# Router logits of the last three tiles as matmuls, and a new order of work between attention and experts

## The chip, the core and the metric

The kernel runs on one core of a Trainium2 chip. A core has five engines, each with its own instruction stream: TensorE (PE, matmuls and transposes, results into PSUM), VectorE (DVE), ScalarE (ACT), GpSimd (POOL) and SyncE (SP, which here only issues transfers). They run in order and meet only through semaphores; transfers issued by SP, ACT or POOL run on 16 shared DMA engines. The metric is device time in microseconds (us), lower is better, and each kernel is run several times.

## What is computed

A gated cross-attention block followed by a mixture of experts: 4 x 2048 tokens of width 512, 16 heads over a context of 77 rows, then for each token the two best of ten experts (eight true ones and two that give nothing).

```python
x = x + tanh(g_xattn) * xattn(layernorm(x), ctx)        # softmax(q k^T) v, w_out, times tanh(gate)
h = layernorm(x)
logits = h @ gate_w.T + gate_b                          # [tokens, 10]
weights, selected = top_k(softmax(logits), 2)
norm_w = weights * (selected < 8), divided by their sum
out = sum over the chosen experts e of norm_w * (h @ expert_w[e] + expert_b[e])
x = x + tanh(g_ffn) * out
```

## The kernel before

Tokens are cut into 64 tiles of 128 (`NT`), 16 tiles to a batch. After a setup the work has two phases, and the order of instructions on every engine is the order in which the Python code emits them (`manual_schedule`).

**Phase 1, attention.** `step(i)` is run for i from -4 to 62 and holds pieces of several tiles: `scores` of tile i+1 (PE), `softmax_exp` and `softmax_div` of it, the transposition of its attention weights by 32 x 32 squares on DVE (`attn_squares`) and by 16 transfers on SP (`attn_move`, line 353), `attend` of tile i-1 (PE, line 360: ten matmuls of 128 x 512 into `po`), its residual x1 (`residual`, written out by SP at line 374), the second layer norm (`norm_stats`, `norm_root`, `norm_shift`, `norm_apply`, which leaves h in a row buffer `rows[i % 9]`), and the router of tile i-2: `gate_logits` makes ten logits by ten DVE instructions at line 382, each a product of h with one broadcast row of `gwb` and a sum; `choose` finds the two best (lines 410 to 423), `ratio` gets their weight (an Exp on ACT, line 430), and on every second tile `weigh`, `place` and `dispatch` count places by two small matmuls (line 453) and scatter the finished rows (512 values of h, two weights, the token number) into two DRAM buffers `hb`, sorted by expert, with four indirect transfers on POOL (line 475).

**Phase 2, experts.** The rows are read back in 118 slots (`M`): 51 blocks and 8 partial sets in pass 0 (first choices), the same number in pass 1 (second choices). `order[n]` holds (pass, table, index); a table of None is a partial set of one expert, gathered by POOL (line 881). A slot goes through

- `slot_load`: read the row block into one of 11 ring buffers, as five transfers on SP, or on SP and ACT from slot 9 on (lines 902 and 905); the address comes from a table in SBUF, `starts`;
- `slot_acc`: gather the present outputs of the slot's tokens (POOL, line 925);
- `slot_tr`: transpose the rows, for a block by one DVE instruction (line 943) into one of six buffers `hTs`, for a partial set by an ACT copy, four PE transposes and another ACT copy (lines 952 to 958), which take two of the same six buffers;
- `slot_pe`: four f32 products with the expert's weights (line 981; the expert's number is read from the table `which`), 8 records in the trace;
- `slot_out`: add the bias, multiply by the weight, add to the gathered output (DVE, lines 989 and 990);
- `slot_put`: scatter the result to the output (POOL, line 997).

Products go to PSUM tiles from two pools of three buffers: even slots to `px`, odd ones to `pe` (pool `mm`, which `po`, the count matmuls `pp` and `pc` also use).

Three tables (`early_table`, `first_table`, `second_table`) say where the blocks of the first 16 slots, of the rest of pass 0 and of pass 1 begin, and `part_table` gives the partial sets.

**The passage** stands at the end of the code. When tile 63's scores are through, PE still has `attend(62)` and `attend(63)`, and the router has tiles 61, 62 and 63 to do. The code emits products 0 and 1, then for each of the two last tiles: gate logits of the tile before on DVE, `attend`, `choose`, residual, norm; then the loop over q = 1..118, which puts out slot q-1, loads slot q+5, transposes slot q+2, and does product and output of slot q. `tail(q)`, at the end of each turn, spreads tile 63's ten gate logits over turns 0 to 4, its `choose` at 5, its dispatch and the first table at 8, the second table at 12, the partial table at 14.

## Time and profile before

| | us |
|---|---|
| median of 8 runs | 1697.81 |
| lowest, highest | 1696.51, 1700.73 |
| the profiled execution, as timed | 1700.13 |
| its span from first to last instruction | 1698.4 |
| PE busy in it | 1645.3 (97%) |
| DVE busy | 1292.6 (76%) |
| ACT busy | 884.2 (52%) |
| POOL busy | 465.6 (27%) |
| PE on the chain that ended last | 85% |

The profile is one execution as the hardware profiler took it. A busy share is the part of the span in which an engine had an instruction running. The chain of waits is followed back from the last instruction: at each step to what released it, or to the instruction before it on its engine. In a timeline, a line gives start, length, engine, source line, operation, the tile that is written and those that are read, how many instructions of one kind were merged, and in brackets the idle time before it with what seems to have ended it. The granted clock is the share of full speed that TensorE's throttle let through. Attention lasts until about 1223 us of the span; the expert products run from there to 1688 us, and the last scatter ends the span.

### The profile page before, as it was taken

What the parts mean: (1) busy time and instruction counts of PE and PEld (TensorE: products, weight loads), DVE (VectorE), ACT (ScalarE), POOL (GpSimd) and SP (SyncE); (2) the same over time, 40 slices, a digit from 0 to 9 for tenths busy, and PEclk for the clock granted to TensorE, in tenths of its full rate; (3) what the DMA queues carried; (4) which work ended last, traced back from release to release, by engine and by line L of the source; (5) the groups of instructions that cost most, each with busy time, mean ns of one, the idle gap of its engine ahead of it and who ended that gap; (6) DMA issues with size and microseconds to landing.
All of it is one profiled execution on the core that took longest, in us unless ns stands there. A gap on an engine that the chain in (4) does not pass through costs nothing.

```text
span 1698.4 us, 23173 instructions
## 1 busy us (share of the span) xinstructions
PE 1645.3 (97%) x4530; PEld 812.8 (48%) x4530; DVE 1292.6 (76%) x3324; ACT 884.2 (52%) x3188; POOL 465.6 (27%) x617
## 2 busy tenths in 40 slices
PE   8898999999999999999999999999978999999996
PEld 6544455454545455454545455454433444444443
DVE  1553899898998989898998989899987564466553
ACT  2564777777776777777776777777510000100001
POOL 4031111121111111121111211121146556465563
PEclk9999999999999999999999999999989999999998
DMA  7477443346533435543333666665467885578751
GB/s 241 169 203 206 113 97 88 87 108 152 152 88 92 106 93 144 149 107 90 93 87 93 166 158 157 154 167 134 95 168 214 248 234 179 154 231 250 232 182 55
DMA packets 484934, 252.07 MB, mean 148 GB/s; under 512 B 369509, under 2 KB 425829, under 8 KB 484529
## 3 DMA queue, kind: packets, MB, share of 16 engines
q1 hardware_dynamic: 423473, 134.77, 33.9%
q0 software_dynamic: 34528, 103.55, 18.6%
q10 hardware_dynamic: 26784, 12.20, 2.9%
q14 instruction: 109, 0.89, 0.2%
q8 instruction: 40, 0.66, 0.2%
HBM read 119.41 MB, written 100.52 MB: 129 GB/s over the span
## 4 chain that ended last, share of the span: by engine, by line
PE 85%; DVE 5%; issue 3%; DMA 2%; SPq 2%; ACT 1%; another core or an unknown queue 1%; DVEq 0%; POOL 0%; POOLq 0%; ACTq 0%
PE po L360 29%; PE sc L281 29%; PE pe L981 11%; PE px L981 10%; PE pkv L519 2%; DVE prod L382 2%; PE xtr L261 2%; PE pv L622 2%; DMA vw_all<-row 1%; SPq L353 1%; DMA gwb<-in_L_ffn_gate_w_dram 1%; PE pm L597 0%; DVE acc L990 0%; PE str L957 0%
## 5 line engine op out<-in xcount | busy, mean ns | idle before, releaser
L360 PE MATMUL po<-vw,aT 128*128 128x512 f32 (+1 forms) x1280 | 562.9, 595 | 5.7 <-DVE attn L327 5.4
L281 PE MATMUL sc<-m_sb,xnT 128*128 128x385 f32 (+1 forms) x1536 | 552.9, 510 | 0.0
L382 DVE CUSTOM_DVE_ANT_0 prod<-row,gwb,gbias 128x512 f32<-128x512 f32 x640 | 477.9, 747 | 24.0 <-DMA gwb<-in_L_ffn_gate_w_dram 6.2
L360 PEld LDWEIGHTS po<-vw,aT 128*128 128x128 f32 (+1 forms) x1280 | 244.3, 191 | 309.0 <-issue 301.7
L281 PEld LDWEIGHTS sc<-m_sb,xnT 128*128 128x128 f32 x1536 | 283.9, 190 | 212.5 <-issue 86.1
L475 POOL DMA_INDIRECT hb<-row,dst x128 | 128.8, 1006 | 752.6 <-DVE nbh_h L250 673.7
L314 ACT ACTIVATE attn<-sc,nmx 128x77 f32<-128x77 f32 x1024 | 316.0, 347 | 33.3 <-DVE nmx L309 27.7
L314 ACT ACTIVATION_READ_ACCUMULATOR attn<-sc,nmx 128x1 f32 x1024 | 233.2, 228 | 0.0
L981 PE MATMUL px<-big,m_sb 128*128 (+1 forms) x472 | 215.8, 600 | 11.7 <-issue 10.3
L981 PE MATMUL pe<-big,m_sb 128*128 (+1 forms) x472 | 217.8, 605 | 5.2 <-DVE m_sb L943 4.2
L981 PEld LDWEIGHTS px<-big,m_sb 128*128 128x128 f32 x472 | 90.1, 193 | 123.3 <-issue 120.4
L981 PEld LDWEIGHTS pe<-big,m_sb 128*128 128x128 f32 x472 | 90.9, 195 | 117.6 <-issue 112.1
L303 DVE TENSOR_REDUCE mx<-sc 128x5 f32<-128x385 f32 (+1 forms) x192 | 106.2, 580 | 19.2 <-PE sc L281 17.1
L233 ACT ACTIVATE sdh_h<-mvh_h,eps_t 128x1 f32<-128x1 f32 x64 | 18.9, 295 | 191.9 <-DVE rsa_a L245 182.6
L989 DVE TENSOR_TENSOR yb<-px,blks 128x512 f32<-128x512 f32 x59 | 40.4, 686 | 92.3 <-issue 45.8
L989 DVE TENSOR_TENSOR yb<-pe,blks 128x512 f32<-128x512 f32 x59 | 40.5, 686 | 79.7 <-issue 37.6
L952 ACT COPY m_sb<-row 128x512 f32<-128x512 f32 x11 | 6.8, 620 | 177.4 <-DVE acc L990 174.3
L997 POOL DMA_INDIRECT out_dram<-acc,row x75 | 76.3, 1018 | 79.2 <-DVE acc L990 54.4
L264 ACT ACTIVATE xnT<-xtr,bet,gam 128x128 f32<-128x128 f32 x256 | 95.4, 452 | 4.5 <-PE xtr L261 4.5
L327 DVE TENSOR_TENSOR attn<-attn,ri 128x1232 f32<-128x1232 f32 x64 | 92.3, 1442 | 5.1 <-DMA aT<-attn 0.8
L373 DVE SCALAR_TENSOR_TENSOR x<-po,gx,x 128x512 f32<-128x512 f32 x64 | 48.0, 750 | 62.7 <-PE pp L453 36.0
L336 DVE STREAM_TRANSPOSE attn<-attn 128x1248 f32<-128x1248 f32 x64 | 94.1, 1471 | 0.0
(163 smaller groups left out, 1539.4 us busy)
## 6 DMA issues: line engine op xcount, KB each, us to landing
aT<-attn SPq DMA_DIRECT2D x768, 40.0 KB
x<-in_x_dram SPq DMA_DIRECT2D x64, 256.0 KB
out_dram<-x SPq DMA_DIRECT2D x64, 256.0 KB
aT<-attn SPq DMA_DIRECT2D x256, 36.0 KB
row<-hb SPq DMA_DIRECT2D x138, 64.0 KB
big<-in_L_ffn_expert_w_dram SPq DMA_DIRECT2D x32, 256.0 KB
row<-hb ACTq DMA_DIRECT2D x118, 64.0 KB
vw<-vw_all SPq DMA_DIRECT2D x9, 768.0 KB
```

The lines of the kernel that those rows point to most:

```text
L264: nc.scalar.activation(xnT[:, c, :], ptr[:, c, :], AF.Identity, bias=bet[:, c : c + 1], scale=gam[:, c : c + 1],)
L281: nc.tensor.matmul(t[:, : n1 - n0], xnTs[i][:, c, :], m_sb[:, c, n0:n1], start=(c == 0), stop=(c == NC - 1),)
L303: nc.vector.tensor_reduce(mx[:, g0:g1], scs[i, g][:, : (g1 - g0) * SK].rearrange("p (h k) -> p h k", k=SK), AX.X, ALU.max,)
L314: nc.scalar.activation(a[:, h * SK : (h + 1) * SK], t[:, k : k + SK], AF.Exp, bias=nm[:, h : h + 1], scale=SCALE, accum_out=sm[:, h : h + 1],)
L327: nc.vector.tensor_tensor(a, a, ri.unsqueeze(2).to_broadcast([P, H, SK]), ALU.mult)
L336: nc.vector.transpose(a[:, :n], a[:, :n])
L360: nc.tensor.matmul(po, aT[:m, k, :], vw[:m, k, :], start=(k == 0), stop=(k == NKC - 1),)
L382: nc.vector.tensor_tensor_reduce(prod, hrs[i][:, :D], gwb[:, e, :], 1.0, gbias[:, e : e + 1], ALU.mult, ALU.add, pgs[i][:, e : e + 1],)
L475: ins = nc.gpsimd.indirect_dma_start(out=hb[k], out_offset=bass.IndirectOffsetOnAxis(ap=dst[:, i % 2, k : k + 1], axis=0), in_=hr[:, :].bi ...
L981: nc.tensor.matmul(pe, hsT[:, c, :], w[:, c, :], start=(c == 0), stop=(c == NC - 1))
L989: nc.vector.tensor_tensor(tt, pe, b, ALU.add)
L997: ins = nc.gpsimd.indirect_dma_start(out=of, out_offset=bass.IndirectOffsetOnAxis(ap=tok, axis=0), in_=acc, in_offset=None, bounds_check=T ...
```

## The change

Six things are changed; phase 1 up to step 61 stays as it was but for one small load and four transposes.

1. `setup_gate` (at step 4): the gate weights, loaded once more as ten rows by SP, are transposed by four small PE transposes and copied to `gwT`. The logits of tiles 61, 62 and 63 are made by `gate_transpose` (four PE transposes of h, one ACT copy to `hgT`) and `gate_product` (four PE products of 10 columns, one DVE instruction that adds the bias) in place of ten DVE instructions for each.
2. The 16 transfers of tile 63's attention weights go alternately to SP and ACT.
3. Row blocks are loaded 8 slots ahead in the loop in place of 5, blocks are transposed 5 slots ahead in place of 2; partial sets still 2 ahead, but into six buffers of their own, `hPs`, in the space of `gwb`.
4. Products 0 to 2 go to `px`, 3 to 5 to `pe`, and so on in threes; the counts `pp` and `pc` of the passage use the transposes' PSUM tiles.
5. In the passage products 1 to 5 stand between the gate steps; all routing of tile 63 is emitted before the output of slot 0, its four scatters one behind each of the outputs 1 to 4 in the program (`later`).
6. The tables are made at turns 3, 6 and 9 in place of 8, 12 and 14.

```diff
-    def attn_move(i, n0=0, n1=16):
-        for dst, src in moves[i][n0:n1]:
-            nc.sync.dma_start(dst, src)
+    def attn_move(i, n0=0, n1=16, queues=(nc.sync,)):
+        for n, (dst, src) in enumerate(moves[i][n0:n1]):
+            queues[n % len(queues)].dma_start(dst, src)
...
+    def setup_gate():
+        rows10 = rows[NRB - 1][:, :D]
+        ptr = tr_tile("gwtr")
+        for c in range(NC):
+            nc.tensor.transpose(ptr[:, c, :NG], rows10[:NG, c * P : (c + 1) * P], ident[:NG, :NG])
+        nc.vector.tensor_copy(gwT, ptr[:, :, :NG])
+
+    def gate_transpose(i):
+        ptr = tr_tile(f"gtr{i}")
+        for c in range(NC):
+            nc.tensor.transpose(ptr[:, c, :], hrs[i][:, c * P : (c + 1) * P], ident)
+        nc.scalar.copy(hgT, ptr)
+
+    def gate_product(i):
+        pl = tr_tile(f"gl{i}")[:, 0, :NG]
+        for c in range(NC):
+            nc.tensor.matmul(pl, hgT[:, c, :], gwT[:, c, :], start=(c == 0), stop=(c == NC - 1))
+        pgs[i] = stile("pg", i, NG)
+        nc.vector.tensor_tensor(pgs[i], pl, gbias, ALU.add)
...
-            attn_move(i + 1)
+            attn_move(i + 1, queues=(nc.sync, nc.scalar) if i + 1 == NT - 1 else (nc.sync,))
...
-        hp, hsT = (hTs[(turn[1] + k) % len(hTs)] for k in range(2))
-        turn[1] += 2
+        hp, hsT = (hPs[(turn[2] + k) % len(hPs)] for k in range(2))
+        turn[2] += 2
...
-        if n % 2:
+        if n // 3 % 2:
             pe = mm_tile(f"pe{n}")
...
     def tail(q):
-        i = NT - 1
-        if q < 5:
-            gate_logits(i, 2 * q, 2 * q + 2)
-        elif q == 5:
-            choose(i)
-            ratio(i)
-        elif q == 8:
-            weigh(i // 2)
-            place(i // 2)
-            pc = count_rows(csum[0][:, 0])
-            dispatch(i // 2)
-            first_table(pc)
-        elif q == 12:
+        if 0 < q <= len(later):
+            put_rows(*later[q - 1])
+        if q == 3:
+            first_table(count_rows(csum[0][:, 0], flat_tr("pclast")))
+        elif q == 6:
             second_table()
-        elif q == 14:
+        elif q == 9:
             part_table()
...
+        nc.sync.dma_start(rows[NRB - 1][:NG, :D], gate_w)
         for i in range(1, NT - 1):
...
-            if i == NT - 2:
-                slot_load(3)
-                slot_load(4)
+            if i == 4:
+                setup_gate()
             step(i)
...
-        slot_load(5)
+        for n in range(3, 6):
+            slot_load(n)
         slot_pe(0)
-        slot_pe(1)
-        slot_tr(2)
-        slot_tr(3)
+        for n in range(1, 3):
+            slot_tr(n)
         for i in (NT - 2, NT - 1):
-            gate_logits(i - 1, 0, NG)
             attend(i)
-            choose(i - 1)
-            ratio(i - 1)
+            gate_transpose(i - 1)
             residual(i)
             norm_stats(f"h{i}", x1s[i])
             norm_root(f"h{i}")
-            if i == NT - 2:
-                weigh(i // 2 - 1)
-                place(i // 2 - 1)
-                dispatch(i // 2 - 1)
+            slot_pe(i - NT + 3)
+            gate_product(i - 1)
             norm_shift(f"h{i}")
             hrs[i] = rows[i % NRB]
             norm_apply(f"h{i}", hrs[i][:, :D], x1s.pop(i))
+            choose(i - 1)
+            ratio(i - 1)
             if i == NT - 2:
-                slot_pe(2)
-                slot_load(6)
+                weigh(i // 2 - 1)
+                place(i // 2 - 1, flat_tr("pp"))
+                dispatch(i // 2 - 1)
+                slot_tr(3)
+                for n in range(6, 9):
+                    slot_load(n)
         for n in range(4):
             slot_acc(n)
-        tail(0)
+        i = NT - 1
+        slot_pe(3)
+        gate_transpose(i)
+        slot_tr(4)
+        slot_pe(4)
+        gate_product(i)
+        choose(i)
+        ratio(i)
+        slot_tr(5)
+        slot_pe(5)
+        weigh(i // 2)
+        place(i // 2, flat_tr("pplast"))
+        dispatch(i // 2, later)
         slot_out(0)
         for q in range(1, M + 1):
-            if 1 < q < M - 5:
-                slot_load(q + 5)
+            if q < M - 8:
+                slot_load(q + 8)
             slot_put(q - 1)
...
-            if 1 < q < M - 2:
-                slot_tr(q + 2)
-            if 2 < q < M:
+            for n, whole_tile in ((q + 5, True), (q + 2, False)):
+                if n < M and whole_tile == (order[n][1] is not None):
+                    slot_tr(n)
+            if 5 < q < M:
                 slot_pe(q)
             if q < M:
                 slot_out(q)
             tail(q)
```

More of the change, by code (lines that the diff above doesn't have):

```diff
@@ L459, in place, with dispatch @@
             )
-    def dispatch(m):
+    def dispatch(m, later=None):
         pos, pp = poss.pop(m), pps.pop(m)
@@ L773, with count_rows @@
     ]
[L774 to L778 removed]
+    hPs = [gwb[:, n, :].rearrange("p (c k) -> p c k", k=P) for n in range(6)]
+    hgT = m_flat[:, 6 * D : 7 * D].rearrange("p (c k) -> p c k", k=P)
+    scr = m_flat[:, 7 * D :]
+    assert NT * (2 * NE + 1) <= NC * COLS - 7 * D
+    def count_rows(cs, pc=None):
+        pc = mm_tile("pc") if pc is None else pc
         nc.tensor.matmul(
```

46 lines of the change are left out of this document (25 added, 21 removed).

## The prediction

> **What bounds the kernel now.** First I read busy time by stretch: start and end in us, length, busy us of TensorE (PE), its weight loads, VectorE (DVE), ScalarE (ACT), GpSimd (POOL), granted clock, DMA share, GB/s.
>
> ```profile
> 1240.00:1260.00 20.00, 15.54 (x36) 6.37 (x34) 14.64 (x47) 5.23 (x8) 8.38 (x8) 0.97 0.53 147
> 1260.00:1280.00 20.00, 14.25 (x30) 6.29 (x31) 18.21 (x39) 1.58 (x2) 14.50 (x14) 0.77 0.76 226
> 1280.00:1300.00 20.00, 19.04 (x48) 8.32 (x47) 16.09 (x39) 0.00 (x0) 13.55 (x14) 1.00 0.79 233
> 1300.00:1350.00 50.00, 45.75 (x100) 19.82 (x99) 31.06 (x57) 0.00 (x0) 27.94 (x28) 0.93 0.83 236
> 1350.00:1500.00 150.00, 145.21 (x358) 65.11 (x357) 76.62 (x113) 9.23 (x16) 88.97 (x87) 0.99 0.66 193
> 1500.00:1650.00 150.00, 150.00 (x357) 66.78 (x356) 90.58 (x132) 1.72 (x3) 95.48 (x92) 1.00 0.78 228
> 1650.00:1698.00 48.00, 35.11 (x93) 16.28 (x91) 12.99 (x18) 7.21 (x13) 21.21 (x21) 0.87 0.23 70
> ```
>
> PE is full from 200 to 1220 us and from 1500 to 1650. So only PE's own work, its idle time and its slow clock set the end. Idle time sits in the passage (1238 to 1311), around 1440 and 1484, and near the end. The PE timeline (start, length, instructions, idle time before) names the places:
>
> ```profile
> 1214.20 8.75 PE L360 MATMUL po<-vw,aT 128*128 128x512 f32 x20
> 1222.79 3.60 PE L981 MATMUL px<-big,m_sb 128*128 x8
> 1252.15 3.60 PE L981 MATMUL pe<-big,m_sb 128*128 x8
> 1265.75 4.51 PE L981 MATMUL px<-big,m_sb 128*128 x6 [10.00 <-issue]
> 1311.06 6.60 PE L981 MATMUL pe<-big,m_sb 128*128 x8 [4.25 <-DVE m_sb L943]
> 1446.21 0.75 PE L957 MATMUL str<-ident,m_sb 128*128 128x128 f32 x4 [2.42 <-ACT m_sb L952]
> 1446.75 5.25 PE L981 MATMUL px<-big,m_sb 128*128 128x512 f32 x8
> 1486.04 3.70 PE L981 MATMUL px<-big,m_sb 128*128 x8 [1.38 <-DVE acc L990]
> 1659.38 1.11 PE L957 MATMUL str<-ident,m_sb 128*128 128x128 f32 x4 [3.52 <-ACT m_sb L952]
> ```
>
> A po, the output of one attention tile, takes 8.59 us from start to start; a slot's product (8 matmuls) 3.43. Wait A is 10.0 us before product 4, wait C 4.25 before product 15, D 2.42 (with 0.99 at 1439.69) and F 3.52 before transposes of partial slots, E 1.38 before product 62. After A, C, D and F the clock is low: product 15 takes 6.44 us start to start. What A and C wait for stands in DVE's timeline:
>
> ```profile
> 1257.12 0.69 DVE L989 TENSOR_TENSOR yb<-px,blks 128x512 f32<-128x512 f32 x1
> 1260.41 0.75 DVE L990 SCALAR_TENSOR_TENSOR acc<-yb,row,acc 128x512 f32<-128x512 f32 x1 [2.60 <-DMA acc<-out_dram,row]
> 1262.80 0.81 DVE L990 SCALAR_TENSOR_TENSOR acc<-yb,row,acc 128x512 f32<-128x512 f32 x1 [0.91 <-DMA acc<-out_dram,row]
> 1264.99 0.71 DVE L943 STREAM_TRANSPOSE m_sb<-row 128x512 f32<-128x512 f32 x1
> ...
> 1305.10 0.75 DVE L990 SCALAR_TENSOR_TENSOR acc<-yb,row,acc 128x512 f32<-128x512 f32 x1
> 1310.12 0.20 DVE L816 TENSOR_SCALAR which<-m_sb 128x64 int32<-128x64 f32 x1
> 1310.29 0.71 DVE L943 STREAM_TRANSPOSE m_sb<-row 128x512 f32<-128x512 f32 x1
> ```
>
> Slot 4's transpose (1264.99) stands behind the outputs of slots 0 and 1, which wait for rows gathered only after the last tile's x is written out. Slot 15's (1310.29) stands behind the second table (1305.77 to 1310.32).
>
> **What the change does to the passage.** From product 0 (1222.79) to product 16 (1317.50) is 94.71 us. Its work is 16 x 3.43 + 2 x 8.59 + 0.2 for five small count matmuls = 72.3; the other 22.4 are waits and low clock. I follow the new instruction order by hand with the durations of before.
>
> Removed: 30 gate products of 0.8 us on DVE (two tiles' runs, 1230.44 to 1238.3 and 1243.27 to 1251.2, then the last tile's ten between slots). They are on the path only through A.
>
> Added on PE, all on the path: per tile four transposes (0.44, as the four from 1430.80 to 1431.24) and four f32 products of 10 columns. No such product is in the trace. A PE group of 4 f32 products has 8 records. Spacing is 0.03 in the 40-column bf16 counts, 0.11 in the transposes, 0.43 in the 512-column products: 0.24, 0.9 or 3.4. The transposes load the same f32 weights, so I take 0.9. Three tiles: 3 x 1.34 = 4.0 (2.0 to 11.5).
>
> New waits on PE, from short DVE and ACT rows: the count matmul of tiles 60 and 61 waits for choose(61) after the new product (bias add 0.2, reciprocal and shift 0.35, max to mask 0.8): 1.4. Product 5 waits for a transpose behind choose(63): 0.2 + 0.95 + 0.7 = 1.9. Product 6 waits for two dispatch steps, slot 0's output and a transpose: 0.4 + 1.4 + 0.7 = 2.6. With the tables moved to slots 3 and 6 DVE catches up nearly in time: 1.0 before product 12 in my list. Sum 6.9. My list in times of the span: product 0 from 1222.8, po62 from 1226.2 (its weights land 1.5 after the last issue at 1224.5), product 1 1235.3, counts 1241.0, po63 1241.1, product 2 1250.2, product 3 1254.5, product 4 1258.4, product 5 1264.6, product 6 1270.7 (before: 1274.4), product 12 about 1292, product 16 about 1306 at full clock. Here DVE stands still at the gate bias add, and the x statistics and transposes queue behind it.
>
> Low clock: D's wait of 2.42 cost 5.08 - 3.43 = 1.65, E's 1.38 nothing. So 1.65 for the wait of 2.6 and half of it for that of 1.9: 2.5 (0 to 3.3).
>
> Passage after: 72.3 + 4.0 + 6.9 + 2.5 = 85.7, so **-9.0**.
>
> The Trainium skill ("TensorE: Matmul & The Clock Gate", Part 1) lets the clock halve only after an idle window of 3.4 us. By that rule the 2.5 would be 0 and the passage -11.5; the 2.42 us of D speak against it, so the row decides.
>
> **Last attn over two queues.** Before, 16 moves go out from 1231.45 to 1241.94 on SP, and po63 starts 1.5 later. In the new order po63 cannot start before 1241.1 anyway, behind the count matmul. One queue from 1228.2, where the earlier transpose lets it begin, would land at 1240.2, two at about 1236. So 0 on the path either way; eight issues (5.2 us) hold ACT to about 1234.3, before it is needed for the gate copy at 1235.3. If that cover goes, up to 5.2. "DMA: Bandwidth & Descriptors" (Issuing engines are not separate DMA queues) says that a second engine saves only issue time; issue time is just what is long here, and by the rule the sum is the same.
>
> **Rows and transposes further ahead.** SP takes loads as ring rows come free, not in step with the products: slot 50's load is issued at 1406.33, its product starts at 1435.11. So plain loads gain 0. Transposes go from 2 to 5 slots ahead; that removes E (-1.4), as product 62's transpose no longer stands behind an output waiting for gathered rows. C is in the passage's sum. Loads 3 to 8 now pass out x62 and x63 on SP: about 3.0 us each from 1233.4, so x63 leaves at about 1251.5, just after it is made (1250.7). Its readers are needed only at 1268. The last tiles' four scatters (1.3 each on POOL) move from 1288.5 on to one behind each of outputs 0 to 3; the rows of slot 16 wait for them and for the first table, which both end before 1290, and are needed at about 1302: 0.
>
> Partial slots (gathered rows): POOL takes three indirect DMAs of 1.32 = 3.96 us per slot there, against a PE slot of 3.43 + 0.44.
>
> ```profile
> 1438.18 1.01 POOL L881 DMA_INDIRECT row<-hb,pidx  x1 [0.31 <-issue]
> 1439.50 1.01 POOL L997 DMA_INDIRECT out_dram<-acc,attn  x1 [0.30 <-issue]
> 1440.81 1.03 POOL L925 DMA_INDIRECT acc<-out_dram,row  x1 [0.30 <-issue]
> 1442.15 1.01 POOL L881 DMA_INDIRECT row<-hb,pidx  x1 [0.30 <-issue]
> 1446.75 1.01 POOL L997 DMA_INDIRECT out_dram<-acc,attn  x1 [3.59 <-DVE acc L990]
> ```
>
> In this run without pauses DVE and ACT see PE's results late (slot 50's product ends at 1438.5, its bias add starts at 1444.99), and D and F come out of that; why is open. Eight gathers move 3 slots earlier, so 2 instead of 5 fall among partial slots, and whole slots are covered by five transposes in hand. D is 0.99 + 2.42 + 1.65 = 5.1, F 3.52 + 2.4 + 0.5 = 6.4. Scaled by 2/5: D 2.0, F 2.6. But ACT's load of slot 59 now stands before slot 53's copy and waits for slot 48's put: +2.3. Net **-4.6** (+2.3 to -11.5).
>
> **Six open products** changes nothing in number: 3 buffers of each pool were in turn before too. Which pool a product takes changes, so that po62 and po63 fit; 0, included above.
>
> Phase 1 gains four transposes of the gate weights: +0.4, PE being full. The extra SP load falls in SP's free 2.2 us after 164.1: 0.
>
> **Sum:** -9.0 - 1.4 - 4.6 + 0.4 = -14.6 on the span of 1698.4, 1683.8. The profiled run took 1700.13 by the clock of the runs, but the span is 0.6 above their median; forecast **1683.2**, say 1683.5.
>
> **Rivals.**
> (1) The wait is only passed on: the gates' products cost 3.4 a tile, D and F stay. For: the PE-ACT-DVE chain of each gate has no slack. Against: A and C are gone by order. 1683.5 + 3 x 2.5 + 4.6 = 1695.6. Chance 0.17, about half of it below 1694.4.
> (2) D and F vanish and the clock holds: 1683.5 - 6.9 - 2.5 = 1674. For: gathers leave the partial stretch; against: why signals are late is unknown. 0.08.
> (3) Slower: the transpose of slot q+5 now stands before output q on DVE, so a late row block holds back every output. Loop of six slots: output 1.4, put 4.0 (issued at 1398.42, its ring row is loaded again at 1402.50), load issue 1.4, landing 2.3 to 5, transpose 0.7 = 9.8 to 12.5, room 20.6. Beyond 20.6 each further 1 us costs 1/6 us on some 100 slots, 16.7 in all; it decides against the gain from 0.9 us on. Price with 1.2 us: 1683.5 + 20 = 1703.5. For it:
>
> ```profile
> 1320.00:1340.00 20.00, 20.00 (x48) 8.92 (x47) 11.98 (x18) 0.00 (x0) 11.64 (x12) 1.00 0.89 250
> ```
>
> at 250 GB/s the DMA engines are close to full, and a slot's 776 KB per 3.43 us are 226. Against: 8 us of room. 0.15.
> (4) The change doesn't do what it says: true of "six open products" and of plain loads, priced 0.
>
> **Chances.** Below about 0.2% (3.4 us) a difference can't be told from none here. Main case 0.60. Faster: 0.60 + 0.08 + 0.09 = 0.77; same 0.08; slower 0.15. The main case alone spans 1677 to 1690. For 8 in 10 I go down to rival 2 and up to rival 1: 1674 to 1696.
>
> **What would show it.** Product 16 starting near 1308.5 instead of 1317.5 shows the passage; no wait of 10 before product 4, waits of 1 to 3 before the counts, products 5 and 6. No wait at product 62. PE idle near the partial slots about half. Gate products spaced far over 0.11, or a wait of DVE transposes for rows in the steady part, would make it wrong.

## The result and the profile after

The changed kernel took 1711.0 us (median of 11 runs, 1701.65 to 1717.08), the kernel before 1698.13 (32 runs) on the same chip: ratio 1.0073, 95% interval 1.0059 to 1.0086. It is slower; the forecast was 1683.5, with 1674 to 1696 as its range. The profiled execution took 1710.21, its span is 1708.5, which is 10.1 over the 1698.4 of before.

Product starts in the two traces (us of the span) tell where; D, E and F are the waits that the prediction named:

| stretch | before | after | difference | forecast |
|---|---|---|---|---|
| start to product 0 (phase 1) | 1222.79 | 1223.55 | +0.8 | +0.4 |
| product 0 to 16 (the passage) | 94.71 | 95.40 | +0.7 | -9.0 |
| product 16 to 59 (D in it) | 156.69 | 166.61 | +9.9 | -0.8 |
| product 59 to 63 (E in it) | 15.38 | 13.73 | -1.65 | -1.4 |
| product 63 to 117, the last (F in it) | 195.47 | 195.97 | +0.5 | -3.8 |

These rows come from one trace of each kernel. In the traces of the experiments below and in these two the old passage takes 91.1 to 94.7 us (the kernel before, b1, e4, e7, e16; 92.7 on average), the changed one 89.1 to 95.8 (the changed kernel, a1, e1, e5, e14; 92.3): it gained next to nothing. When both kernels were profiled once more on one chip (b1 and a1), the 10.3 us between their spans were +2.3, +3.5, +3.9, -1.35 and +1.8 on these five rows. So how the loss divides between the stretches is known only roughly.

The same view by stretch as before (start and end, length, busy us of PE, its weight loads, DVE, ACT, POOL, granted clock, DMA share, GB/s), for the changed kernel:

```profile
1240.00:1260.00 20.00, 18.70 (x56) 9.23 (x56) 6.46 (x29) 6.63 (x8) 4.11 (x5) 0.91 0.54 141
1260.00:1280.00 20.00, 15.58 (x45) 7.51 (x44) 9.67 (x26) 1.19 (x4) 8.53 (x9) 0.91 0.51 142
1280.00:1300.00 20.00, 19.98 (x47) 8.46 (x46) 17.39 (x42) 0.00 (x0) 15.43 (x16) 1.00 0.70 225
1300.00:1350.00 50.00, 44.17 (x97) 19.20 (x97) 28.49 (x46) 0.00 (x0) 30.26 (x29) 0.93 0.76 223
1350.00:1500.00 150.00, 138.80 (x339) 62.93 (x338) 76.59 (x112) 9.53 (x16) 90.11 (x87) 0.97 0.69 198
```

PE has 18.70 busy us of the first 20 where it had 15.54, and 15.58 where it had 14.25: the ten idle us before product 4 are gone. But from 1300 to 1350 it is 44.17 (45.75 before), from 1350 to 1500 138.80 (145.21).

PE's timeline of the changed kernel (start, length, instructions, idle time before):

```profile
1239.74 0.96 PE L412 MATMUL gl<-gwT,m_sb 128*128 128x10 f32 x8
1241.79 0.19 PE L476 MATMUL pp<-msk,upper 128*128 128x40 bf16 x1 [1.09 <-DVE msk L435]
...
1242.21 10.52 PE L360 MATMUL po<-vw,aT 128*128 128x512 f32 x20 [0.21 <-issue]
...
1267.48 5.13 PE L1012 MATMUL pe<-big,m_sb 128*128 x8 [1.88 <-DVE w L463]
...
1275.21 10.57 PE L1012 MATMUL px<-big,m_sb 128*128 x24 [2.54 <-DVE m_sb L974]
...
1309.27 6.41 PE L1012 MATMUL px<-big,m_sb 128*128 x8 [5.83 <-DVE m_sb L974]
```

The same view at the partial slots of pass 0:

```profile
1436.12 0.60 PE L988 MATMUL str<-ident,gwb 128*128 128x128 f32 x4
...
1444.93 1.12 PE L988 MATMUL str<-ident,gwb 128*128 128x128 f32 x4 [4.56 <-ACT gwb L983]
1445.84 4.62 PE L1012 MATMUL pe<-big,gwb 128*128 128x512 f32 x8
1457.10 1.12 PE L988 MATMUL str<-ident,gwb 128*128 128x128 f32 x4 [6.64 <-ACT gwb L983]
```

Three waits of the passage are those of the forecast: 1.09 before the counts (1.4), 1.88 before product 5 (1.9), 2.54 before product 6 (2.6); the gate's group of eight records takes 0.96 (0.9). The fourth wait of the forecast, 1.0 before product 12, is absent; 5.83 before product 14 was not forecast, and low clock follows it (6.41 us long instead of 3.60). At the partial slots 4.56 and 6.64 stand where 0.99 and 2.42 stood. What product 14 waited for is in DVE's timeline:

```profile
1298.97 0.71 DVE L974 STREAM_TRANSPOSE m_sb<-row 128x512 f32<-128x512 f32 x1 [1.52 <-DMA row<-hb]
...
1308.50 0.71 DVE L974 STREAM_TRANSPOSE m_sb<-row 128x512 f32<-128x512 f32 x1 [7.08 <-DMA row<-hb]
```

A whole block's transpose waits for its rows, for 7.08 us. In the loop the same wait comes 36 more times, 56.0 us in all (0.4 in the kernel before), and PE stays full there. (The expectations speak of 52 us: so much of it, with the passage's, is on `row` tiles.)

### The profile page after: what moved, and what is told of

It reads as the page before. It is cut to its first block, busy times and chain, and to the rows that moved or that the text cites. A ratio compares the mean times of both kernels' runs of the same rounds, so it can differ in the third digit from the quotient of the medians.

```text
span 1708.5 us, 23205 instructions
## 1 busy us (share of the span) xinstructions
PE 1652.5 (97%) x4570; PEld 819.3 (48%) x4570; DVE 1270.3 (74%) x3268; ACT 885.7 (52%) x3191; POOL 467.4 (27%) x617
## 5 line engine op out<-in xcount | busy, mean ns | idle before, releaser
L382 DVE CUSTOM_DVE_ANT_0 prod<-row,gwb,gbias 128x512 f32<-128x512 f32 x610 | 455.4, 747 | 22.7 <-DMA gwb<-in_L_ffn_gate_w_dram 7.4
L1012 PE MATMUL px<-big,m_sb 128*128 x424 | 190.3, 603 | 8.4 <-DVE m_sb L974 8.4
L1012 PE MATMUL pe<-big,m_sb 128*128 x392 | 173.0, 597 | 1.9 <-DVE w L463 1.9
L1012 PEld LDWEIGHTS px<-big,m_sb 128*128 128x128 f32 x424 | 81.4, 194 | 110.0 <-issue 99.4
L1012 PEld LDWEIGHTS pe<-big,m_sb 128*128 128x128 f32 x392 | 74.8, 192 | 95.2 <-issue 92.1
L327 DVE TENSOR_TENSOR attn<-attn,ri 128x1232 f32<-128x1232 f32 x64 | 92.3, 1442 | 5.0 <-DMA aT<-attn 0.8
L983 ACT COPY gwb<-row 128x512 f32<-128x512 f32 x11 | 6.8, 619 | 167.8 <-DMA row<-hb,pidx 162.3
L956 POOL DMA_INDIRECT acc<-out_dram,row x75 | 80.4, 1072 | 36.5 <-issue 22.2
```

Of the source, the lines that this page charges most:

```text
L327: nc.vector.tensor_tensor(a, a, ri.unsqueeze(2).to_broadcast([P, H, SK]), ALU.mult)
L382: nc.vector.tensor_tensor_reduce(prod, hrs[i][:, :D], gwb[:, e, :], 1.0, gbias[:, e : e + 1], ALU.mult, ALU.add, pgs[i][:, e : e + 1],)
L956: ins = nc.gpsimd.indirect_dma_start(out=acc, out_offset=None, in_=of, in_offset=bass.IndirectOffsetOnAxis(ap=tok, axis=0), bounds_check=T ...
L1012: nc.tensor.matmul(pe, hsT[:, c, :], w[:, c, :], start=(c == 0), stop=(c == NC - 1))
```

## The experiments

Theory 1: the gathers of the partial slots, moved three slots ahead, crowd GpSimd where whole slots run. Theory 2: whole-block transposes, five ahead on VectorE, wait for rows and hold outputs and puts. Theory 3: the passage gains nothing. Theory 4 came out of the first two calls. All ratios are to the kernel before, run in the same call. "Run" is a stretch in which GpSimd issues indirect DMAs with no pause over 0.45 us.

| run | median us | ratio, 95% interval |
|---|---|---|
| e1_gathers_back | 1700.74 | 1.0037 (1.0021 to 1.0053) |
| e2_transposes_back | 1703.66 | 1.0057 (1.0039 to 1.0076) |
| e3_loop_as_before | 1699.02 | 1.0027 (1.0013 to 1.0042) |
| e4_before_with_loop | 1698.76 | 1.0028 (1.0012 to 1.0044) |
| e5_passage_alone | 1697.22 | 1.0012 (1.0000 to 1.0025) |
| e7_gathers_spread | 1685.99 | 0.9949 (0.9932 to 0.9966) |
| e8_outputs_earlier | 1698.07 | 1.0028 (1.0013 to 1.0044) |
| e9_ring_of_14 | 1700.28 | 1.0033 (1.0014 to 1.0051) |
| e10_changed_gathers_spread | 1687.74 | 1.0048 (1.0034 to 1.0062) |
| e11_outputs_earlier_gathers_spread | 1688.24 | 1.0049 (1.0035 to 1.0063) |
| e12_outputs_earlier_old_loop_spread | 1675.59 | 0.9976 (0.9967 to 0.9985) |
| e13_outputs_earlier_old_loop | 1676.22 | 0.9979 (0.9969 to 0.9989) |
| b1_before_again | 1693.90 | 0.9997 (0.9984 to 1.0010) |
| a1_changed_again | 1705.53 | 1.0050 (1.0033 to 1.0066) |
| e13b_outputs_earlier_old_loop | 1693.74 | 0.9996 (0.9984 to 1.0008) |
| e14_changed_gathers_spread | 1693.02 | 0.9984 (0.9964 to 1.0005) |
| e16_gathers_bunched | 1692.84 | 0.9986 (0.9974 to 0.9999) |
| e17_outputs_earlier_old_loop_spread | 1690.72 | 0.9973 (0.9961 to 0.9985) |

The kernel before took 1694.8 to 1695.2 us in the first, second, fourth and fifth call (1698.1 beside the result) and 1679.75 in the third, that of e10 to e13; each call ran on another chip.

### First call: one part of the loop at a time

e1 and e2, against the changed kernel:

```diff
-            if q < M - 8:
-                slot_load(q + 8)
+            for n, is_block in ((q + 8, True), (q + 5, False)):
+                if n < M and n > 8 and is_block == (order[n][1] is not None):
+                    slot_load(n)
```
```diff
-            for n, whole_tile in ((q + 5, True), (q + 2, False)):
-                if n < M and whole_tile == (order[n][1] is not None):
-                    slot_tr(n)
+            if 3 < q < M - 2:
+                slot_tr(q + 2)
```

e3 has e2's edit and all loads at q + 5 from q = 4. e4 is the kernel before with the changed loop (and buffers of their own for the partial slots) from slot 20 on.

> The changed kernel, with only the gathers of the sixteen partial slots issued five slots ahead again (blocks stay eight ahead, transposes five). Theory 1 (the gathers, moved three slots earlier, make GpSimd's run without pauses at the partial slots of pass 0 11 us longer, and TensorE loses there about 10 us more): waits and low clock between products 50 and 58 go back to about 5 us; from product 16 to 59 about 10 us less than the changed kernel's 166.6; time near 1701. Theory 2 (the whole-block transposes, five ahead on VectorE, wait for rows and hold outputs and puts back; that makes the loss at product 14 and at the partial slots): nothing moves, 1709 to 1712.

> The changed kernel, with only the whole-block transposes two slots ahead again (loads and gathers stay eight ahead). Theory 1: the wait before product 14 (5.8 us and about 2.8 of low clock) goes, the loss at the partial slots stays: 1702 to 1704, and product 16 to 59 stays at 166 or so. Theory 2: both go, 1692 to 1694, and the 52 us that VectorE's transposes waited for rows fall below 5.

> The changed kernel with the loop's rows and transposes as before (all loads five ahead, all transposes two ahead); the passage, the gates as matmuls and the two queues stay. What is left is the worth of the passage alone. If the passage's order brought what was forecast and only the loop lost (both theories): product 16 near 1310 instead of 1319, product 16 to 59 near 157, time 1688 to 1692. Rival theory 3 (the passage itself gains nothing, since its new waits and low clock of 9 us take the place of the one removed): 1697 to 1700.

> The kernel before, with the changed loop (loads and gathers eight ahead, whole-block transposes five ahead, own buffers for the partial slots) from slot 20 on; the passage is untouched. Theories 1 and 2: the loop alone loses what the changed kernel lost between products 16 and 63, about 8 to 10 us: 1706 to 1708. Theory 3 (the loop is harmless, the loss comes over from the passage, whose late puts push GpSimd's work towards the partial slots): 1697 to 1699.

In e1 the loads from slot 67 on go over ring rows whose slots are not done, so part of pass 1 is computed from other rows and its total can't be used; its pass 0 is as meant. There the waits at the partial slots are 1.47, 5.48, 0.92 and 2.61, 10.5 in all, against 11.2 in the changed kernel: putting the gathers back alone does not help, which speaks against theory 1 by itself. In e2 and e3 they fall to 4.6 and 4.1, as theory 2 has it, but both kernels have a new wait of 11.5 before product 6, because its transpose now stands behind the first table on VectorE: five ahead is needed in the passage as it was rebuilt. This wait is also why their times, 1703.66 and 1699.02, lie where theories 1 and 3 had put them; that agreement is luck. In e4 the loop alone costs 1.0028, about half of the loss (1.0073, and 1.0050 in the fourth call), with 2.49 + 2.81 at the partial slots of pass 0 and 4.92 in pass 1. No single part of the loop is the loss.

### Second call: the passage, the outputs, the ring, and the gathers out of the way

e5 is the changed kernel up to slot 20 and the old loop after it. e7 takes the kernel before and spreads the gathers of the partial slots, each into a row of its own:

```diff
+        if t is None:
+            hs = gwb.rearrange("p e d -> p (e d)")[:, s * ROW : (s + 1) * ROW]
...
-            if 1 < q < M - 5:
+            if 1 < q < M - 5 and order[q + 5][1] is not None:
                 slot_load(q + 5)
+            for first, early in ((half - NE, 18), (M - NE, 66)):
+                if q - early in range(0, 4 * NE, 4):
+                    slot_load(first + (q - early) // 4)
```

e8 is the changed kernel with outputs 0 to 2 ahead of the last gate, the last x written ahead of loads 6 to 8, and the late scatters two slots later; e9 is the changed kernel with three more ring rows in the free part of `gwb`:

```diff
         slot_pe(4)
+        for n in range(3):
+            slot_out(n)
         gate_product(i)
...
-        if 0 < q <= len(later):
-            put_rows(*later[q - 1])
+        if 2 < q <= len(later) + 2:
+            put_rows(*later[q - 3])
```
```diff
+    spare = gwb.rearrange("p e d -> p (e d)")[:, 6 * D :]
+    ring += [spare[:, v * ROW : (v + 1) * ROW] for v in range(3)]
```

> The changed kernel with the loop of before (loads five ahead, transposes two ahead, shared buffers, the old choice of pools) from slot 20 on; the passage up to there, with its transposes five ahead, is the changed one. The run with the whole loop as before had a wait of 11.48 us before a product of the passage, because transposes then stand behind the first table; that wait should be gone here. Theory 2 (loss in the loop by transposes that wait for rows on VectorE, gain in the passage given back at product 14): product 16 near 1318, partial slots as before (about 5 us of waits and low clock), ratio to before 1.000 to 1.002 (0 to +3 us). Theory 3 (passage worse by itself): 1.004 and more. If the wait before product 14 is chance: ratio 0.995.

> The kernel before, with the gathers of the sixteen partial slots taken out of the stretch where GpSimd has three indirect DMAs a slot: own rows in the place of the gate weights, one gather every four slots, from slot 18 and from slot 66. If GpSimd's run without pauses makes the waits at the partial slots (in the kernel before 0.99 + 2.42 and 3.52 us with the low clock after them), they go: 7 to 11 us less, ratio 0.994 to 0.996. If the waits come from the partial slots' own chain (copy, transpose by TensorE, copy on ScalarE), they stay: ratio 0.999 to 1.001.

> The changed kernel, with loads 6 to 8 issued after the write of the last x tile on SyncE, outputs 0 to 2 on VectorE ahead of the last tile's gate, and the four late scatters behind puts 2 to 5 instead of 0 to 3. If the wait before product 14 (5.83 us, then 2.8 of low clock) comes from puts that start late (1274.8, before 1261.6) and free the rows of the ring late: puts start near 1265, the wait goes, 8 us less than the changed kernel, ratio about 1.002 (1.0073 - 0.005); partial slots of pass 0 unchanged. If it also carries over to the partial slots: ratio 0.997. If the row wait has another cause, or outputs 0 to 2 hold the last gate back by as much: 1.006 to 1.009.

> The changed kernel with three more rows in the ring (14 for 11), in the part of the gate weights that the partial slots leave free. Theory 2 (a slot's row is free only when an older slot's put has read it; with loads eight ahead in a ring of eleven the row comes too late for a transpose five ahead): the 52 us of VectorE's waits for rows fall below 10, the wait before product 14 goes, and the partial slots fall back to 5 us: 15 us less, ratio 0.998. Theory 1 (gathers moved into GpSimd's crowded stretch): row waits fall, the 10 us at the partial slots stay, ratio 1.003. If rows are late by the transfers themselves (DMA engines 0.8 busy): nothing moves, 1.007.

e7 beats both kernels, by 0.5%. At the partial slots nothing is left to wait for: no idle time over 0.6 us on PE between 1409 and 1476, nor after 1477. Its row of the stretch with the partial slots of pass 0 (columns as above):

```profile
1420.00:1500.00 80.00, 78.25 (x206) 35.78 (x205) 40.41 (x59) 9.23 (x16) 44.87 (x44) 1.00 0.62 174
```

PE is busy for 78.25 of 80 us at full clock (75.21 at 0.98 before, 68.80 at 0.94 in the changed kernel). So in the kernel before the place of the gathers, not the partial slots' own chain, made D and F.

e8 reaches the length that was forecast for the passage: product 14 does not wait, product 16 starts 85.0 us after product 0 (1221.83 to 1306.81; forecast 85.7). It still loses to the kernel before (1.0028), because the partial slots take the gain back:

```profile
1428.29 3.60 PE L1012 MATMUL pe<-big,gwb 128*128 128x512 f32 x8
1444.07 1.12 PE L988 MATMUL str<-ident,gwb 128*128 128x128 f32 x4 [12.18 <-issue]
1444.97 4.89 PE L1012 MATMUL pe<-big,gwb 128*128 128x512 f32 x8
```

12.18 us instead of 4.56 + 6.64. What holds e8 here is ScalarE. The loop now has it issue its part of a later block before it copies the rows of a partial slot; ACT's timeline of e8:

```profile
1429.04 14.26 ACTq L936 DMA_DIRECT2D attn<-hb  x2
1443.39 0.62 ACT L983 COPY gwb<-row 128x512 f32<-128x512 f32 x1 [14.32 <-DMA row<-hb]
```

Between the two transfers of one block ACT stands for 13.4 us, until one that SP issued at 1439.66 has landed, and the copy for the transposes of 1444.07 stands behind them. The prediction had this order as a term ("ACT's load of slot 59 now stands before slot 53's copy", +2.3). In the changed kernel's first trace no such hold lies before these copies, in its second (a1) one of 3.9 us does.

In e9, with three more ring rows, transposes no longer wait for rows in the passage (1.53 and 0.84 within product 13 are left on PE) and in pass 1 (20.6 us in the changed kernel), so there the size of the ring bears on the waits. Between product 16 and 59 they still wait 32.5 us (35.4), and 14.80 stand at the partial slots: there rows are not late for want of ring rows alone. e5 keeps a wait of 2.33 before product 14 and gets a new one of 3.24 in the loop (1364.40); it ends level, as theory 2 had it.

Theory 4, from here: rows, outputs and puts come late where GpSimd runs without pauses, and the change lengthens these runs. In the kernel before they are 15.7 us in the passage (1288.5 to 1304.2) and 24.1 at the partial slots of pass 0; in the changed kernel 30.2 (1274.8 to 1305.0) and 35.2 (1417.3 to 1452.5). The passage's run gets longer since outputs 0 to 3, held back to 1273, release their puts at once and the last scatters stand among them.

### Third call

e10 and e11 spread the gathers in the changed kernel and in e8; e13 is e8's passage with the old loop from slot 20, e12 the same with the gathers spread. In e10 and e11 the copies of a partial slot go over the buffer that the product two slots earlier has yet to read, so these products have other rows.

> The changed kernel with the sixteen gathers of the partial slots spread as in the kernel before (own rows in the gate weights' place, one every four slots; two buffer pairs for their copies). Theory 4 (the change's loss sits where a gather stands on GpSimd behind puts, and the puts behind outputs that wait for rows on VectorE): the waits at the partial slots (4.56, 6.64 and 5.24 us, with the low clock after them some 20 us) go; ratio 1.0073 - 0.0115 = 0.996, near the 0.9949 that the kernel before reaches with its gathers spread. If the loss is not in that order: D and F stay, 1.004 to 1.007.

> The changed kernel with outputs 0 to 2 earlier, and the gathers spread too. The run with outputs earlier lost 12.18 and 4.29 us at partial slots (some 20 us with the low clock). Theory 4: both go, and its passage of about 86 us shows in the time at last: ratio 1.0028 - 0.0115 = 0.991. If the late outputs of the loop only move the wait to another place: 0.996 to 1.0.

> The changed passage with outputs 0 to 2 earlier, the loop of before from slot 20 on, and the gathers spread. The sum of two parts measured alone: the passage about 9 us shorter (86 for 94.7) and the partial slots 8.7 us shorter (0.9949 alone): ratio 0.989 to 0.991. If the passage's gain is worth nothing at the end: 0.995.

> The same without the spread: the changed passage with outputs 0 to 2 earlier and the loop of before from slot 20 on. If the gain of the passage is lost in the changed loop alone: 9 us less than before, ratio 0.9945. If the partial slots take it back also in the old loop (GpSimd there sets the time, whatever comes ahead): 0.998 to 1.0, with longer waits at the partial slots of pass 0 than the 3.4 us of before.

On this chip the kernel before took 1679.75, and the waits that the call was to tell apart were absent: e13 waits 4.9 us on PE in the whole second phase (24.2 before on the first chip), none of it at partial slots, and spreading brings nothing (e12 against e13: 1675.59 and 1676.22). Yet GpSimd runs without pauses there too, from 1279.7 to 1340.3 and from 1406.5 to 1444.3. POOL's timeline of e13 in that second run (idle time before each in brackets):

```profile
1434.08 1.01 POOL L912 DMA_INDIRECT row<-hb,pidx  x1 [0.31 <-issue]
1435.39 1.00 POOL L1028 DMA_INDIRECT out_dram<-acc,attn  x1 [0.30 <-issue]
1436.70 1.03 POOL L956 DMA_INDIRECT acc<-out_dram,row  x1 [0.30 <-issue]
```

PE of e13 at the same time:

```profile
1434.19 3.60 PE L1012 MATMUL pe<-big,m_sb 128*128 128x512 f32 x8
1437.63 0.60 PE L988 MATMUL str<-ident,m_sb 128*128 128x128 f32 x4
```

And DVE's bias add:

```profile
1437.83 0.69 DVE L1020 TENSOR_TENSOR yb<-pe,blks 128x512 f32<-128x512 f32 x1 [2.40 <-PE pe L1012]
```

The product ends at 1437.63, where the next PE instruction starts, and its bias add begins 0.20 later. The passage of e13 is 84.9 us from product 0 to 16. The ratio of 0.9979 is what the passage with its earlier outputs is worth on this chip; the kernel before was not profiled on it, so what its own waits are there is not known. e10 and e11 lose 1.0 us per partial product (4.87 apart for 3.87) to their buffers, so their ratios tell nothing of the rest.

### Fourth call: both kernels and two variants on one chip

The kernel before and the changed one once more, e13 again, and e14: the changed kernel with its gathers spread as in e7 and three buffer pairs in `vw`'s place.

> The kernel before, unchanged, for a profile from the same chip as the next three. If this chip is like the first ones: waits of 3.4 and 3.5 us at the partial slots, passage of 94.7 us from product 0 to 16, ratio 1.000. If it is like the one that took 1679.75: no waits at the partial slots, and the passage tells whether the waits of 10.0 and 4.25 us before products 4 and 15 are there too.

> The changed kernel, unchanged. On a chip like the first ones: 1.006 to 1.009, with about 11 us of waits at the partial slots of pass 0. On a chip like the one that took 1679.75: no waits at the partial slots; if the loss belongs to those waits alone, the passage decides and the ratio is 0.994 to 0.999; if the transposes' waits for rows lose it in any case, 1.003 or more.

> The changed passage with outputs 0 to 2 earlier and the loop of before from slot 20 on, once more. 0.9979 on the chip that took 1679.75. On a chip like the first ones, where the kernel before loses 10 us in wait A and 4 in wait C: passage 86 us for 94.7, ratio 0.994 to 0.996 if the partial slots don't take it back, 0.998 to 1.0 if they do.

> The changed kernel with the gathers of the partial slots spread (one every four slots, own rows) and three buffer pairs for their copies, in the place of vw. On a chip like the first ones, theory 4: the waits at the partial slots go (some 20 us with the low clock), ratio 0.995 to 0.998. On a chip like the one that took 1679.75, where there are no such waits: the same time as the changed kernel within 0.1%.

This chip is like the first ones, and the changed kernel loses again: 1.0050. Its row waits in the passage fall on products 14 and 15 (0.99 and 4.54), its waits at partial slots are 1.99 + 7.71 and 0.79 + 4.33 (before: 5.57 and 3.04), its longest runs 30.2, 38.0 and 32.4 us (before: 18.3, 24.1, 28.1). e14 takes 0.66% off that (1.0050 to 0.9984); in pass 1 it has no wait at partial slots left, in pass 0 still 7.71 + 1.89, after a run of 27.1 us (1413.7 to 1440.8) that comes about without the gathers. Of the 16.0 us between the traces of a1 and e14, 7.8 come from pass 1 and 8.2 from phase 1 and the passage, where e14 changes nothing; product 16 to 59 takes 163.4 and 163.8. So the gathers' place is not what makes the changed kernel's loss in pass 0.

e13b shows what becomes of the passage's gain. Product 16 starts at 1307.1, 6 us ahead of the kernel before on this chip (1313.2). But output 20 starts at 1330.48, against 1330.59: rows of slots 18 and 19 come late at the end of a run of 27.5 us, and PE, which had products in hand, stands still later. DVE's transposes of these rows in e13b:

```profile
1308.38 0.71 DVE L974 STREAM_TRANSPOSE m_sb<-attn 128x512 f32<-128x512 f32 x1 [5.23 <-DMA attn<-hb]
...
1314.33 0.71 DVE L974 STREAM_TRANSPOSE m_sb<-attn 128x512 f32<-128x512 f32 x1 [3.55 <-DMA attn<-hb]
```

PE's wait in e13b:

```profile
1345.08 6.67 PE L1012 MATMUL px<-big,m_sb 128*128 x8 [3.46 <-DVE m_sb L974]
```

3.46 of wait and 3.2 of low clock: the 6 us are gone.

### Fifth call: the run without pauses by itself

e16 is e7 with the gathers of pass 0 bunched again, one a slot, but among whole slots and 15 slots or more before anyone needs them. e17 is e12 on another chip.

```diff
-            for first, early in ((half - NE, 18), (M - NE, 66)):
-                if q - early in range(0, 4 * NE, 4):
-                    slot_load(first + (q - early) // 4)
+            for first, early, every in ((half - NE, 28, 1), (M - NE, 66, 4)):
+                if q - early in range(0, every * NE, every):
+                    slot_load(first + (q - early) // every)
```

> The kernel before with its sixteen gathers in own rows, those of pass 1 spread as in the run that reached 0.9949, those of pass 0 bunched again, but among whole slots (28 to 35, one each), 15 to 23 slots before their rows are used. The work is the same; only GpSimd's pauses go there (three indirect DMAs a slot for eight slots). Theory 4 (a run of GpSimd without pauses holds back what other engines and queues get to see): waits of 3 to 8 us of TensorE, and outputs that start several us after their products end, near slots 28 to 40; ratio 0.998 to 1.000. Rival (gathers cost only because the partial slots need their rows at once): no wait there, ratio 0.994 to 0.996.

> The changed passage with outputs 0 to 2 earlier, the old loop from slot 20 on, and all gathers spread (0.9976 on the chip where the kernel before took 1679.75 us). On a chip like the others: the spread brings 8.7 us, as in the kernel before; the passage 3 to 6 us if what it saves on TensorE lasts, ratio 0.991 to 0.993; 0.995 to 0.997 if the loop gives it back as it did without the spread (0.9996).

e16 speaks for theory 4. Up to 1352.3 GpSimd pauses for 1.10 us in every slot, then no longer; POOL's timeline of e16:

```profile
1352.34 0.99 POOL L1000 DMA_INDIRECT out_dram<-acc,row  x1 [1.10 <-DMA row<-hb]
1353.64 1.04 POOL L928 DMA_INDIRECT acc<-out_dram,attn  x1 [0.30 <-issue]
1354.99 1.42 POOL L884 DMA_INDIRECT gwb<-hb,pidx  x1 [0.31 <-issue]
1356.71 1.02 POOL L1000 DMA_INDIRECT out_dram<-acc,attn  x1 [0.30 <-issue]
...
1371.50 1.01 POOL L884 DMA_INDIRECT gwb<-hb,pidx  x1 [0.31 <-issue]
1375.76 1.01 POOL L1000 DMA_INDIRECT out_dram<-acc,row  x1 [3.24 <-DVE acc L993]
```

PE of e16, products of whole slots:

```profile
1364.12 3.60 PE L984 MATMUL pe<-big,m_sb 128*128 x8
1367.55 3.60 PE L984 MATMUL px<-big,m_sb 128*128 x8
...
1376.16 3.70 PE L984 MATMUL px<-big,m_sb 128*128 x8 [1.57 <-DVE acc L993]
```

DVE of e16, the bias adds of three of them:

```profile
1360.89 0.69 DVE L992 TENSOR_TENSOR yb<-pe,blks 128x512 f32<-128x512 f32 x1 [1.33 <-issue]
...
1366.12 0.69 DVE L992 TENSOR_TENSOR yb<-px,blks 128x512 f32<-128x512 f32 x1 [3.14 <-remote]
...
1374.00 0.69 DVE L992 TENSOR_TENSOR yb<-pe,blks 128x512 f32<-128x512 f32 x1 [5.78 <-remote]
```

The bias add of 1360.89 starts 0.2 after its product, as is usual. That of the product which ends at 1367.55 starts at 1374.00, 6.4 late, "remote", after GpSimd has stopped at 1372.5 (it then waits 3.24 for an output). PE waits 1.57 and, after the next run, 2.06 for free product buffers, where 3 to 8 were expected. Nothing but the place of eight gathers differs from e7 in pass 0, and the ratio is 0.9986 for 0.9949. The two ran on different chips, so the size is rough: of the 7.5 us between their traces 4.5 lie between product 16 and 59, and 2.8 behind product 63, where the two kernels are alike.

A run without pauses does not cost by its length alone. e7 has one of 27.9 us among whole slots (1377.4 to 1405.4), and DVE shows the same lateness at its end, the product having ended at 1401.1:

```profile
1406.70 0.69 DVE L992 TENSOR_TENSOR yb<-pe,blks 128x512 f32<-128x512 f32 x1 [6.40 <-remote]
```

PE waits only 0.88 us after it. Full DMA engines alone do not make the lateness either: in the kernel before they are 0.89 busy from 1320 to 1340, where GpSimd pauses, and no bias add between 1305 and 1438 is over 0.6 us late. So, by these traces, a late output costs where PE runs out of products in hand or of free buffers, and at a partial slot, whose copies stand between PE's transposes and its product.

e17 gives the passage's gain back as e13b did (0.9973; 0.995 to 0.997 was expected if it does): runs of 30.3 and 34.7 us from 1284.3 to 1354.8, then waits of 1.41 and 5.62 at 1349 and 1358.

What stays open: that the longer run is what makes row 14 late in the passage is argued from e16 and from the run's length, and was not tried in the passage by itself (e8, with a run of 27.5 us there, kept PE supplied and paid at the partial slots); why results and rows come late during such runs; whether GpSimd's missing pauses as such do it or something in its transfers; and why one chip of those tried shows nothing of it.

## Why the prediction was wrong

The direction was wrong. The steps that failed are the partial slots' term and, in the passage, C. By its steps:

- **The bound.** "PE is full from 200 to 1220 us and from 1500 to 1650. So only PE's own work, its idle time and its slow clock set the end." This holds for the whole kernel, not in the passage: there the chain row, transpose, product, output, put, row sets it, and PE runs up to six products ahead of it. e13b shows it: product 16 six us earlier, output 20 not at all.
- **The passage, -9.0.** Three of the four new waits came as forecast. The length of 85.7 was reached only with outputs 0 to 2 placed earlier (e8: 85.0, e13: 84.9), an order that the prediction did not follow, so this agreement is in part luck. The step that failed here is C: "Slot 15's (1310.29) stands behind the second table". Moving the table took that order away, but the outputs of that place were already late, one bias add until 1304.37, the end of GpSimd's run of 15.7 us. In the changed kernel this run is 30.2 us, and a wait came back as 5.83 before product 14 with 2.8 of low clock (in the five traces with this passage the longest wait before products 14 to 16 is 2.3 to 5.8). That the longer run makes it is argued, as said above. Another 1.8 is po63 at low clock (10.36 from start to start for 8.59) after the wait of 1.09, which the sum had free.
- **Low clock.** "1.65 for the wait of 2.6 and half of it for that of 1.9": the same wait of 1.88 before product 5 cost 1.5 us in the changed kernel (5.13 long) and nothing in e1, e5 and e14 (3.70 long), so half of it was a fair mean. The wait of 2.54 before product 6, for which the sum had 1.65, cost nothing in the changed kernel (3.70 long) and 1.6 in e5. The Trainium skill ("TensorE: Matmul & The Clock Gate", Part 1) calls the gate's window free-running, so that the point of change varies from run to run; the rows agree with that, while its idle window of 3.4 us is longer than any of these waits.
- **Partial slots, -4.6.** This step failed most: the stretch with D grew by 9.9 us (3.9 in the fourth call's pair) where -0.8 was forecast. "Eight gathers move 3 slots earlier, so 2 instead of 5 fall among partial slots, and whole slots are covered by five transposes in hand" scaled D and F by the gathers' place and took the early transposes for cover. Both halves failed. With the gathers back in their old place (e1) the waits at the partial slots of pass 0 are 10.5 us and GpSimd's run 35.7, with the gathers gone from there (e14) 9.6 us. And the transposes are no cover: they wait for rows themselves, 56.0 us in the loop. All six traces with the changed passage (e8 has outputs 0 to 2 earlier in it) and transposes five ahead through the loop wait 9.6 to 14.8 us there (the changed kernel, a1, e1, e8, e9, e14); with only one of the two it is 3.4 to 5.3 (e2, e3, e4, e5, e13b), in the kernel before 3.4 and 5.6, and with the old loop and the gathers spread nothing (e7, e16 and e17). All these are traces from the chips that show the lateness. So the growth takes both together; why both are needed stays open. The text said of the late results "why is open" and still took them for a cost of the partial slots alone.
- **E, -1.4:** -1.65 measured. **Phase 1, +0.4:** +0.8, within what this stretch varies from run to run (product 0 at 1219.4 to 1223.8 in all kernels). **Two queues, loads, six open products, 0 each:** no wait of the traces points to them but one of 1.02 us in e12, where po63 waits for its attention weights.
- **Rivals.** Rival 3 named the right mechanism, transposes that wait for a late row block, but its price was wrong: it took 20.6 us of room in a loop through the ring. The waits came (56.0 us in the loop), PE hid nearly all of them, and more ring rows (e9) do not remove those of pass 0. That they cost by bunching outputs, and so GpSimd's DMAs, is a reading of the traces that no run tried by itself. Of rival 1, D and F stayed, and grew.

## What to carry to other kernels

Before work is moved on TensorE, look for the engine that issues DMAs without pauses in that stretch, and count its instructions per slot against the slot's time: a queue at 3.96 us per 3.43 falls behind, and in these runs, on every chip but one, other engines then got results late that were in time by their own order. Transfers that are needed late and can be issued any time (here sixteen gathers of the kernel before, 0.5%) belong where that queue has pauses. A stretch shortened on the busiest engine is a gain only if the chain that gives its buffers back gets shorter too.

## What was not expected of the hardware

While GpSimd issued indirect DMAs with pauses of 0.30 us only, other engines acted on finished work late. In the sixteen traces from the chips that show this, 131 bias adds start over 1 us after both their product and DVE's instruction before them have ended; 127 of these products ended in a run of 10 us or more. Two places stand for them: a bias add 6.4 us after its product (e16), and ScalarE's copies in the changed kernel 6.1 and 8.8 us after the transposes by PE that they read. The profile names their releaser "remote" or not at all. ACT's timeline there:

```profile
1442.77 0.59 ACT L989 COPY gwb<-str 128x512 f32<-128x512 f32 x1 [6.85 <-remote]
...
1454.84 0.58 ACT L989 COPY gwb<-str 128x512 f32<-128x512 f32 x1 [9.96 <-remote]
```

POOL's at that time:

```profile
1451.47 1.02 POOL L956 DMA_INDIRECT acc<-out_dram,row  x1 [0.30 <-issue]
1456.54 1.01 POOL L1028 DMA_INDIRECT out_dram<-acc,attn  x1 [4.05 <-DVE acc L1021]
```

The transposes before the copy of 1442.77 ended at 1436.72 (1436.12 + 0.60), those before that of 1454.84 at 1446.05 (1444.93 + 1.12); the second copy, like the bias add of e16, came only after GpSimd had stopped (1452.49). What is late is the signal. Each engine tells others of finished work by raising a semaphore, and the traces keep records of these rises. In e16 TensorE's semaphore rises at 1373.98 and 1374.07, for products that ended at 1367.7 and 1371.1, and the bias add starts at 1374.00; in the changed kernel it rises at 1442.74 and 1454.75, and the copies start at 1442.77 and 1454.84. Late rises often come several together, 0.1 us apart. On these chips only about half to three quarters of the rises have a record, so this can't be followed for each of them.

On one chip runs of 60.6 us (e13) and 84.7 (e12) did none of this: every rise has a record there, and up to the last product none is more than 0.3 us late. The kernel before was about 1% faster on it.
